# Four-layer graph network on one core: adding some gathered near rows on GpSimd between the gathers

## The chip, the core and the metric

The kernel runs on one core of one Trainium2 chip. The metric is the device time of one execution in microseconds (us); the figure given for a kernel is the median of its runs. A profiled execution has a time of its own and, a little shorter, a span from the first to the last instruction in the trace; all places in time below are microseconds from the start of that span.

Engines are named as in the profile: PE is TensorE (matrix products), DVE is VectorE, ACT is ScalarE, POOL is GpSimd, SP is SyncE (it only issues DMA transfers here).

## What is computed

There are N = 2708 nodes with D = 128 features and a dense adjacency matrix `adj`. Four layers follow one another, each on `h = relu(layernorm(x))`, each adding its result to `x`. The change lies in the second half of the first layer:

```python
d  = 1 / sqrt(sum(A, axis=-1))
z  = leaky_relu((d * (A @ (d * h))) @ W1 + b1, 0.1)     # first product with A
S  = exp(-sqrt(|z_i - z_j|^2 + 1e-10) / 2)              # all pairs of nodes
S  = where(rank of S in its row < 4, S, 0)              # four nearest of each node
A2 = S + A
d2 = 1 / sqrt(sum(A2, axis=-1))
x  = x + (d2 * (A2 @ (d2 * h))) @ W2 + b2               # second product
```

`S` has four nonzero entries in a row. So `A2 @ y` is the dense product `A @ y` plus, for each node, four rows of `y`, picked by index and weighed by `S`. Layer 1 is an attention layer that needs all of the new `x`; layers 2 and 3 are two more products with `adj`.

## The kernel before

**Tiles.** The nodes are cut into T = 22 tiles of 128 (the last has 20). `xs[:, t, :]` is tile t of `x`, 128 x 128 in float32, and stays in SBUF. `adj` comes in transposed; `chunk(i)` is a band of 128 of its rows, 1354 KB, loaded by SP's queue. GROUPS are the six groups of four tiles (the last has two); a group's 512 columns of a product fill one PSUM bank.

**Second product.** After the four nearest of each node are known (`top_i`, `top_v`), `y2 = dinv2 * (h @ W2)` is written to SBUF and to a table in HBM, `ydr`. Two things then run side by side.

- `aggregate(y2, done_l0, ...)` (line 388; matmuls recorded at L400) is the dense product. For the first 17 bands PE multiplies one band into all six banks while SP loads the next; the last five bands are kept in SBUF and are multiplied bank by bank, so that the banks become complete one after the other. For each of the first four complete banks `done_l0` runs `to_x1`: ACT copies the bank to `u2T` (L968), PE transposes it (L378), DVE scales it and adds it to `xs` (L962). Then `layernorm_relu` makes `h1` of the group. The last two groups, `E4` (tiles 16 to 19) and `E5` (tiles 20 and 21), are written out by hand below (`x1`, `moments`, `roots`, `scales`, `normed` and so on).
- The four near rows of every node are gathered from `ydr`. `gathered(idx)` (L918) issues one indirect DMA on POOL's queue: 128 indices, one row of 512 bytes for each partition, 64 KB. POOL works out its descriptors. There are 85 of them: four for each of the tiles 0 to 20, and one (`last_four`) for the 20 nodes of tile 21. The destination is one of 23 buffers `gath`. `add_near(t)` adds them: DVE does `xs[t] = gath * simd[t, k] + xs[t]`, once for each k (L929; L84 where the order is written by hand).

**Order.** Gathers stand on POOL in the order of the tiles, one after another. DVE's adds of the tiles 0 to 14 stand ahead of everything that `done_l0` does. Those of the tiles 15, 16, 17 and 18 stand in `done_l0` of the groups 0, 1, 2 and 3, behind that group's layernorm. Tile 19 (`T - 3`) follows by hand, then `x1(E4)` and `x1(E5)`. The four rows of tile 20 (`T - 2`) are weighed and added on POOL itself (L1029, L1030), behind the last gather:

```python
for g, k in zip(near_late[T - 2], range(TOPK)):
    pin(nc.gpsimd.tensor_scalar(g, g, simd[:, T - 2, k : k + 1], None, op0=ALU.mult))
    pin(nc.gpsimd.tensor_tensor(xs[:, T - 2, :], g, xs[:, T - 2, :], ALU.add))
```

`pin(...)` and the engines `pe`, `dve`, `act` keep instructions in the order of the program on their engine; other instructions are placed by a scheduler. Each engine works through its instructions in order, and one that waits holds up all behind it. `last_four` reaches `xs` of tile 21 by a small product with `four_w` (L1164 to L1170).

**What follows.** `x1(E5)` adds the dense part to the tiles 20 and 21; from there DVE and ACT go on to the layernorms of `E4` and `E5`, `rows_of`, the maximum `rmax` over all nodes and `w_n`. The whole next layer (masks, `total`) reads `rmax` or `w_n`.

Of the kernel before, what the change touches and what calls it, by code (L numbers as in the profile page):

```python
# [12 lines left out]
ALU = mybir.AluOpType  # L13
# [5 lines left out]
TOPK = 4  # L19
# [5 lines left out]
def kernel(  # L25
# [18 lines left out]
    nc = tc.nc  # L44
    N, D = x.shape
    assert D == P
    T = -(-N // P)
# [25 lines left out]
    def pin(ins):  # L73

        return tc.keep_in_program_order(ins)
# [10 lines left out]
    pe, dve, act = Ordered(nc.tensor), Ordered(nc.vector), Ordered(nc.scalar)  # L86
# [26 lines left out]
    def spread(y, queue):  # L113

        for g in range(1, 4):
            queue.dma_start(y[32 * g : 32 * g + TAIL, T - 1, :], y[:TAIL, T - 1, :])
# [16 lines left out]
    xs = keep.tile([P, T, D], F32, name="xs")  # L133
# [101 lines left out]
    with nc.allow_non_contiguous_dma(reason="256 elements"):  # L235
# [16 lines left out]
        out=above, in_=ones_b, pattern=[[1, P]], compare_op=ALU.is_ge, fill=0.0, base=-1, channel_multiplier=-1  # L252
# [17 lines left out]
    for v, first, fill in ((1, 3, float(P // 2)), (2, 2, -1e5)):  # L270
        nc.gpsimd.affine_select(
            out=empty[:, v, :], in_=empty[:, v, :], pattern=[[0, T]],
# [3 lines left out]
            out=empty[:, v, :], in_=empty[:, v, :], pattern=[[-PER, T]],  # L276
# [42 lines left out]
    def layernorm_relu(dst, g):  # L319

        t0, t1 = GROUPS[g]
        n = t1 - t0
        st = small.tile([P, 4, 6], F32, name="ln_st")
        mv = small.tile([P, 4, 2], F32, name="ln_mv")
        rs = small.tile([P, 4], F32, name="ln_rs")
        for t in range(t0, t1):
            nc.vector.bn_stats(st[:, t - t0, :], xs[:, t, :])
            nc.vector.bn_aggr(mv[:, t - t0, :], st[:, t - t0, :])
        root = nc.scalar.activation(rs[:, :n], mv[:, :n, 1], AF.Sqrt, bias=ln_eps)
        nc.vector.reciprocal(rs[:, :n], rs[:, :n])  # L330
        nm = small.tile([P, 4], F32, name="ln_nm")
        nc.vector.scalar_tensor_tensor(
            nm[:, :n], mv[:, :n, 0], -1.0, rs[:, :n], op0=ALU.mult, op1=ALU.mult
        )
        for t in range(t0, t1):
            o = t - t0
            nc.scalar.activation(
                dst[:, t, :],
                xs[:, t, :],
                AF.Relu,  # L340
                scale=rs[:, o : o + 1],
                bias=nm[:, o : o + 1],
            )
        return root
# [43 lines left out]
    def aggregate(y, done, more=None, kept=0, back=1, first=1):  # L388

        out = [acc(b) for b in range(NKB)]
        last = T - pools["n"]

        def product(i, b):
            k0, n = KBS[b]
            r = slice(32 * (b % 4), 32 * (b % 4) + TAIL) if i == T - 1 else slice(0, P)
            nc.tensor.matmul(  # L400
                out[b][:, :n],
                y[r, i, :],
                chunk(i)[r, k0 : k0 + n],
                start=(i == 0),
                stop=(i == T - 2),
            )

        for i in range(last):
            if more is not None:
                more(i)  # L410
            resident[i] = chunk(i)
            if i > 2 and T - 1 in resident and pools["apart"]:
                last_rows()
            for b in range(NKB):
                product(i, b)
            if i < last - kept:
                del resident[i]
            if i >= back and (i - back) % 2 == 0:
                absent = [j for j in range(last, T) if j not in resident]
                for j in absent[: first if i == back else 1]:  # L420
                    chunk(j)
        if more is not None:
            for i in range(last, T):
                more(i)
        for b in range(NKB):
            product(T - 1, b)
        for b in range(NKB):
            for i in range(last, T - 1):
                product(i, b)
            if b:  # L430
                done(b - 1, out)
        done(NKB - 1, out)
# [356 lines left out]
    for t in range(T):  # L789
# [4 lines left out]
        for bs in (range(4), range(4, NKB)):  # L794
# [7 lines left out]
            for b in bs:  # L802
                k0, n = KBS[b]
                g = 32 * (b % 4)
# [18 lines left out]
    near_u = res.tile([P, T, TOPK], U32, name="near_u")  # L823
# [33 lines left out]
    ydr = dram.tile([P * T, D], F32, name="ydr")  # L857
# [39 lines left out]
    simd = res.tile([P, T, TOPK], F32, name="simd")  # L897
# [6 lines left out]
    near_p = res.tile([P, 1], U32, name="near_p")  # L904
# [8 lines left out]
    nc.vector.tensor_tensor(four_w, four_w, ident[:, 64:96], ALU.add)  # L913
    nc.vector.tensor_tensor(four_w, four_w, ident[:, 96:128], ALU.add)

    def gathered(idx):
        g = res.tile([P, D], F32, name="gath", bufs=23)
        nc.gpsimd.indirect_dma_start(  # L918
            out=g[: idx.shape[0], :],
            out_offset=None,  # L920
            in_=ydr[:, :],
            in_offset=bass.IndirectOffsetOnAxis(ap=idx, axis=0),
        )
        return g

    def add_near(t, engine=nc.vector):
        for k in range(TOPK):
            g = gathered(near_u[:, t, k : k + 1])
            engine.scalar_tensor_tensor(  # L929
                xs[:, t, :],  # L930
                g,
                simd[:, t, k : k + 1],
                xs[:, t, :],
                op0=ALU.mult,
                op1=ALU.add,
            )
            engine = nc.vector if engine is nc.vector else dve

    def vec(name, n=T, dt=F32):
        return keep.tile([P, n], dt, name=name)
# [17 lines left out]
    def to_x1(g, s2):  # L966
        k0, n = KBS[g]
        nc.scalar.copy(u2T[:, k0 : k0 + n], s2[g][:, :n])  # L968
        node_product(u2T, None, g, add_l0)
# [4 lines left out]
    def terms(g):  # L974

        t0, t1 = GROUPS[g]
        k0, n = KBS[g]
        if not r_ps:
            r_ps.append(acc(0))
        transposed(hT, h1, g, nc.scalar.copy)  # L980
        p = ps_s.tile([P, 512], F32, name="ps")
        nc.tensor.matmul(p[:, :n], rep, hT[:, k0 : k0 + n], start=True, stop=True)
        nc.scalar.copy(row_all[:, k0 : k0 + n], p[:, :n])
        for t in range(t0, t1):
            nc.tensor.transpose(
                r_ps[0][: width(t), t : t + 1], row_all[:1, cols(t)], ident[:1, :1]
            )
        nc.vector.tensor_copy(r_nat[:, t0:t1], r_ps[0][:, t0:t1])
# [16 lines left out]
    def done_l0(g, s2):  # L1005
        if g >= NG - 2:
            complete.append(s2[g])
            return
        to_x1(g, s2)
        layernorm_relu(h1, g)  # L1010
        for t in late[g]:
            add_near(t, dve)
        if g:
            terms(g - 1)

    for t in range(15):
        add_near(t)
    aggregate(y2, done_l0, lambda i: spread(y2, nc.sync) if i == 4 else None, kept=4, back=5)

    E4, E5 = NG - 2, NG - 1

    near_late = {
        t: [gathered(near_u[:, t, k : k + 1]) for k in range(TOPK)] for t in (T - 3, T - 2)
    }
    last_four = gathered(near_p)
    for g, k in zip(near_late[T - 2], range(TOPK)):
        pin(nc.gpsimd.tensor_scalar(g, g, simd[:, T - 2, k : k + 1], None, op0=ALU.mult))  # L1029
        pin(nc.gpsimd.tensor_tensor(xs[:, T - 2, :], g, xs[:, T - 2, :], ALU.add))  # L1030
    for g, k in zip(near_late[T - 3], range(TOPK)):
        dve.scalar_tensor_tensor(
            xs[:, T - 3, :],
            g,
            simd[:, T - 3, k : k + 1],
            xs[:, T - 3, :],
            op0=ALU.mult,
            op1=ALU.add,
        )

    turned = []
    for g, s2 in zip((E4, E5), complete):
# [907 lines left out]
```

## Time and profile before

| | us |
|---|---|
| median of 15 runs | 1108.15 (1103.31 to 1119.15) |
| the profiled execution, its time | 1106.0 |
| its span | 1104.3 |
| first gather starts on POOL | 299.00 |
| last gather (`last_four`) starts | 404.48 |
| POOL's last add of tile 20 ends | 410.12 |
| PE busy, whole span | 995.6 (90%) |
| DVE busy | 582.8 (53%) |
| ACT busy | 401.3 (36%) |
| POOL busy | 209.1 (19%) |

An engine's busy time is an average over stages with different limits. Here only the stage from 291 to 425 matters: the second product, the gathers beside it, and the tail in which the last groups are finished. In a row of the trace's order of time the first two numbers are start and duration, and the bracket holds the idle time of the engine before it and what ended that.

### The profile page before, as it was taken

The numbers are of one execution on the slowest core, as the hardware profiler recorded it, in microseconds if no ns is written. First come the engines' busy times: TensorE is split into PE (matmuls) and PEld (weight loads), VectorE is DVE, ScalarE is ACT, GpSimd is POOL, SyncE is SP. The second block draws the span as 40 slices with busy tenths as digits, with TensorE's granted clock in tenths as the row PEclk, the third lists the DMA queues.
The fourth block names the chain that finished last, engine by engine and source line by source line (L and its number), as shares of the span: only waits on it lengthen the run. The fifth ranks groups of instructions, "written<-read, shape, count | busy, mean of one in ns | idle before, by whom it ended". The sixth has DMA issues, their size and how long they took to land.

```text
span 1104.3 us, 10114 instructions
## 1 busy us (share of the span) xinstructions
PE 995.6 (90%) x3551; PEld 487.6 (44%) x3551; DVE 582.8 (53%) x1185; ACT 401.3 (36%) x625; POOL 209.1 (19%) x199
## 2 busy tenths in 40 slices
PE   7999999999998998899787367777999999999998
PEld 5444444444343455454343133333444455455444
DVE  4365368999842267847466489998310321032003
ACT  6010045444300056668775288786200210021000
POOL 2000000000177760023333145551000000000000
PEclk9999999999998997899999769999999999999999
DMA  9987220004399525889999899999999257715811
GB/s 287 335 313 231 82 70 13 0 1 166 110 366 400 182 90 232 373 325 423 421 419 416 293 421 430 429 431 394 393 352 387 93 207 273 262 64 210 304 42 51
DMA packets 48995, 284.09 MB, mean 257 GB/s; under 512 B 6815, under 2 KB 18171, under 8 KB 29333
## 3 DMA queue, kind: packets, MB, share of 16 engines
q1 hardware_dynamic: 38191, 189.13, 45.6%
q0 software_dynamic: 10512, 94.32, 21.1%
q8 instruction: 28, 0.46, 0.2%
q14 instruction: 24, 0.19, 0.0%
q10 hardware_dynamic: 240, 0.00, 0.0%
HBM read 251.44 MB, written 33.00 MB: 258 GB/s over the span
## 4 chain that ended last, share of the span: by engine, by line
PE 67%; DMA 18%; DVE 8%; ACT 4%; issue 2%; POOL 0%; SPq 0%; DVEq 0%; POOLq 0%; ACTq 0%
PE acc L400 32%; PE acc L84 16%; PE acc L797 10%; DMA pair<-table,pair_u 8%; DMA mov<-in_adj_dram,src_u 5%; PE ps L84 4%; DVE att L84 3%; DMA chunk<-in_adj_dram 2%; PE ps L380 1%; ACT att L84 1%; DVE top_i L834 1%; DMA held<-in_adj_dram 1%; PE acc L805 1%; ACT sg L1510 1%; DVE mask L84 1%
## 5 line engine op out<-in xcount | busy, mean ns | idle before, releaser
L84 PE MATMUL acc<-att,xw 128*128 128x512 f32 (+2 forms) x264 | 110.2, 569 | 54.2 <-DVE att L84 54.1
L400 PE MATMUL acc<-chunk,h 128*128 128x512 f32 (+1 forms) x384 | 148.0, 542 | 0.0
L84 PE MATMUL acc<-mov,wt 128*128 128x512 f32 (+1 forms) x264 | 109.5, 561 | 18.4 <-DVE mov L84 18.2
L918 POOL DMA_INDIRECT gath<-ydr,near_u x84 | 79.9, 951 | 191.5 <-issue 179.6
L797 PE MATMUL acc<-zT 128*128 128x512 f32 (+2 forms) x264 | 112.3, 559 | 0.0
L400 PEld LDWEIGHTS acc<-chunk,h 128*128 128x128 f32 x384 | 68.8, 190 | 74.1 <-issue 74.1
L84 PEld LDWEIGHTS acc<-att,xw 128*128 128x128 f32 (+1 forms) x264 | 49.8, 196 | 114.6 <-issue 82.3
L400 PE MATMUL acc<-chunk,y 128*128 128x512 f32 x204 | 82.8, 568 | 7.9 <-DMA chunk<-in_adj_dram 7.1
L84 PEld LDWEIGHTS acc<-mov,wt 128*128 128x128 f32 x264 | 47.4, 191 | 79.8 <-DVE mov L84 45.9
L812 ACT COPY strip<-acc 128x512 f32<-128x512 f32 (+1 forms) x132 | 60.4, 558 | 59.2 <-issue 35.8
L1735 POOL DMA_INDIRECT pair<-table,pair_u x22 | 64.0, 2911 | 79.2 <-DVE att L84 44.7
L84 DVE SCALAR_TENSOR_TENSOR att<-pair,kap 128x2708 f32<-128x2708 f32 (+3 forms) x24 | 67.1, 2803 | 22.0 <-DMA pair<-table,pair_u 21.3
L84 DVE COPY mov<-knots 2x512 f32<-2x512 f32 x126 | 47.2, 399 | 50.7 <-DMA mov<-in_adj_dram,src_u 23.8
L400 PE MATMUL acc<-chunk,attended 128*128 128x512 f32 x192 | 73.1, 542 | 0.0
L84 ACT ACTIVATE att<-att,sca 128x2708 f32<-128x2708 f32 (+3 forms) x24 | 56.7, 2362 | 41.3 <-DVE att L84 41.3
L84 DVE SCALAR_TENSOR_TENSOR att<-row_all,inv_s,att 128x2708 f32<-128x2708 f32 (+3 forms) x24 | 67.2, 2798 | 4.0 <-ACT att L84 4.0
L814 DVE MAX8 top_v<-strip 128x8 f32<-128x2708 f32 (+1 forms) x22 | 64.6, 2964 | 7.3 <-ACT strip L812 7.3
L797 PEld LDWEIGHTS acc<-zT 128*128 128x128 f32 (+1 forms) x264 | 45.1, 185 | 51.3 <-issue 43.8
L400 PEld LDWEIGHTS acc<-chunk,y 128*128 128x128 f32 x204 | 38.4, 198 | 52.2 <-issue 47.4
L84 ACT ACTIVATE att<-att,hb 128x2708 f32<-128x2708 f32 (+3 forms) x24 | 56.7, 2364 | 0.8
L1510 ACT ACTIVATE sg<-row_all,c_nat 128x2708 bf16<-128x2708 f32 (+1 forms) x22 | 56.4, 2564 | 0.1
L84 ACT COPY knots<-acc 128x512 f32<-128x512 f32 x66 | 37.3, 595 | 40.5 <-PE acc L84 40.4
(355 smaller groups left out, 1244.4 us busy)
## 6 DMA issues: line engine op xcount, KB each, us to landing
chunk<-in_adj_dram SPq DMA_DIRECT2D x75, 1354.0 KB
table<-knots SPq DMA_DIRECT2D x19, 1354.0 KB
res<-in_adj_dram SPq DMA_DIRECT2D x9, 1354.0 KB
held<-in_adj_dram SPq DMA_DIRECT2D x11, 512.0 KB
held<-in_adj_dram SPq DMA_DIRECT2D x16, 256.0 KB
upper<-in_adj_dram SPq DMA_DIRECT2D x4, 842.0 KB
held<-in_adj_dram SPq DMA_DIRECT2D x3, 1024.0 KB
chunkY<-in_adj_dram SPq DMA_DIRECT2D x2, 1354.0 KB
```

What stands on the lines that cost most here:

```text
L84: return lambda *a, **k: pin(getattr(self.engine, name)(*a, **k))
L380: mm = nc.tensor.matmul(p[: width(t), t - t0, :], srcT[:, cols(t)], w, start=True, stop=True)
L400: nc.tensor.matmul(out[b][:, :n], y[r, i, :], chunk(i)[r, k0 : k0 + n], start=(i == 0), stop=(i == T - 2),)
L797: mm = nc.tensor.matmul(zz[b][:w, :n], zT[:, cols(t)], zT[:, k0 : k0 + n], start=True, stop=False)
L805: nc.tensor.matmul(zz[b][:w, :n], ones_b[g : g + 3, :w], sq_rows[g : g + 3, k0 : k0 + n], start=False, stop=True,)
L812: copied = nc.scalar.copy(s[:w, k0 : k0 + n], zz[b][:w, :n])
L814: nc.vector.max(top_v[:w, t, :], s[:w, :])
L834: pin(nc.vector.max_index(top_i[:w, t, :], top_v[:w, t, :], strips[t][:w, :]))
L918: nc.gpsimd.indirect_dma_start(out=g[: idx.shape[0], :], out_offset=None, in_=ydr[:, :], in_offset=bass.IndirectOffsetOnAxis(ap=idx, axis=0),)
L1510: nc.scalar.activation(sg[:w, :], row_all[:w, :], AF.Sign, bias=c_nat[:w, t : t + 1], accum_out=signs[:w, t : t + 1],)
L1735: nc.gpsimd.indirect_dma_start(out=r[:w].rearrange("p a n -> p (a n)"), out_offset=None, in_=table[:, :], in_offset=bass.IndirectOffsetOnA ...
```

## The change

Of each of the tiles 3 to 14, 16 and 18, the fourth near row is no longer added by DVE. For the tiles 3 to 14 (`SHARED`) ACT multiplies it by its weight in place, and POOL adds it to `xs`. For the tiles 16 and 18 (`ALONE`) POOL does both. POOL's part, `join`, is kept in the list `waiting` and is issued ahead of the fourth gather after the tile's own last one, so three gathers stand between the gather of a row and the add of it. All gathers and joins are pinned to the order of the program. The gathers of the tiles 15 to 20 and of tile 21 are now issued in the program ahead of `aggregate`; on POOL they stand in the same order as before. In all 14 adds (12 of `SHARED`, 2 of `ALONE`) leave DVE, 12 multiplications come to ACT, and 14 adds and 2 multiplications come to POOL. As recorded by the program, POOL has 19 gathers, the add of tile 3, four gathers, the add of tile 4, and so on. On ACT the 12 multiplications stand ahead of the first copy to `u2T`.

```diff
+    waiting = []
+
     def gathered(idx):
+        if waiting and waiting[0][0] <= 0:
+            waiting.pop(0)[1]()
+        for v in waiting:
+            v[0] -= 1
         g = res.tile([P, D], F32, name="gath", bufs=23)
-        nc.gpsimd.indirect_dma_start(
...
+        pin(
+            nc.gpsimd.indirect_dma_start(
...
-    def add_near(t, engine=nc.vector):
-        for k in range(TOPK):
-            g = gathered(near_u[:, t, k : k + 1])
+    SHARED, ALONE = range(3, 15), (16, 18)
+
+    def near_rows(t):
+        rows_ = [gathered(near_u[:, t, k : k + 1]) for k in range(TOPK)]
+        if t in SHARED or t in ALONE:
+            g, s_ = rows_.pop(), simd[:, t, TOPK - 1 : TOPK]
+            if t in SHARED:
+                nc.scalar.mul(g, g, s_)
+
+            def join():
+                if t in ALONE:
+                    pin(nc.gpsimd.tensor_scalar(g, g, s_, None, op0=ALU.mult))
+                pin(nc.gpsimd.tensor_tensor(xs[:, t, :], g, xs[:, t, :], ALU.add))
+
+            waiting.append([3, join])
+        return rows_
+
+    def add_near(t, rows_, engine=nc.vector):
+        for k, g in enumerate(rows_):
             engine.scalar_tensor_tensor(
                 xs[:, t, :],
                 g,
...
         for t in late[g]:
-            add_near(t, dve)
+            add_near(t, near_late[t], dve)
...
-    for t in range(15):
-        add_near(t)
+    near_late = {}
+    for t in range(T - 3):
+        rows_ = near_rows(t)
+        if t < 15:
+            add_near(t, rows_)
+        else:
+            near_late[t] = rows_
+    near_late.update((t, near_rows(t)) for t in (T - 3, T - 2))
+    last_four = gathered(near_p)
     aggregate(y2, done_l0, lambda i: spread(y2, nc.sync) if i == 4 else None, kept=4, back=5)
...
-    near_late = {
-        t: [gathered(near_u[:, t, k : k + 1]) for k in range(TOPK)] for t in (T - 3, T - 2)
-    }
-    last_four = gathered(near_p)
     for g, k in zip(near_late[T - 2], range(TOPK)):
         pin(nc.gpsimd.tensor_scalar(g, g, simd[:, T - 2, k : k + 1], None, op0=ALU.mult))
         pin(nc.gpsimd.tensor_tensor(xs[:, T - 2, :], g, xs[:, T - 2, :], ALU.add))
-    for g, k in zip(near_late[T - 3], range(TOPK)):
...
+    add_near(T - 3, near_late[T - 3], dve)
```

More of the change, by code (lines that the diff above doesn't have):

```diff
@@ L914 @@
     nc.vector.tensor_tensor(four_w, four_w, ident[:, 96:128], ALU.add)
+    waiting = []
     def gathered(idx):
+        if waiting and waiting[0][0] <= 0:
+            waiting.pop(0)[1]()
+        for v in waiting:
+            v[0] -= 1
         g = res.tile([P, D], F32, name="gath", bufs=23)
[L918 to L922, printed above, removed]
-        )
-        return g
-    def add_near(t, engine=nc.vector):
-        for k in range(TOPK):
-            g = gathered(near_u[:, t, k : k + 1])
+        pin(
+            nc.gpsimd.indirect_dma_start(
+                out=g[: idx.shape[0], :],
+                out_offset=None,
+                in_=ydr[:, :],
+                in_offset=bass.IndirectOffsetOnAxis(ap=idx, axis=0),
+            )
+        )
+        return g
+    SHARED, ALONE = range(3, 15), (16, 18)
[13 more added lines that the diff above has]
+        for k, g in enumerate(rows_):
             engine.scalar_tensor_tensor(
@@ L1011, in done_l0 @@
         for t in late[g]:
-            add_near(t, dve)
+            add_near(t, near_late[t], dve)
         if g:
             terms(g - 1)
-    for t in range(15):
-        add_near(t)
+    near_late = {}
[7 more added lines that the diff above has]
+    last_four = gathered(near_p)
+    assert not waiting
     aggregate(y2, done_l0, lambda i: spread(y2, nc.sync) if i == 4 else None, kept=4, back=5)
     E4, E5 = NG - 2, NG - 1
-    near_late = {
-        t: [gathered(near_u[:, t, k : k + 1]) for k in range(TOPK)] for t in (T - 3, T - 2)
-    }
-    last_four = gathered(near_p)
     for g, k in zip(near_late[T - 2], range(TOPK)):
@@ L1030 @@
         pin(nc.gpsimd.tensor_tensor(xs[:, T - 2, :], g, xs[:, T - 2, :], ALU.add))
-    for g, k in zip(near_late[T - 3], range(TOPK)):
[L1032 to L1039, printed above, removed]
+    add_near(T - 3, near_late[T - 3], dve)
     turned = []
```

## The prediction

> **What bounds the stage now.** I first asked the profile's page for the gathers and for PE's share of this product, because the change adds work between gathers.
>
> ```profile
> L918 POOL DMA_INDIRECT gath<-ydr,near_u x84 | 79.9, 951 | 191.5 <-issue 179.6
> L400 PE MATMUL acc<-chunk,y 128*128 128x512 f32 x204 | 82.8, 568 | 7.9 <-DMA chunk<-in_adj_dram 7.1
> ```
>
> The busy share of POOL (19% of the span) hides that POOL is full here. From the first gather's start (299.00) to the last one's (404.48) there are 84 steps in 105.48 us: 1.256 us each, of which 0.944 is the gather and 0.30 a gap that follows it. No gather waits longer than this gap for anything. PE, beside it, waited 7.1 us for bands of `adj`.
>
> Next I read the order of time at the end of the stage, POOL first and then DVE.
>
> ```profile
> 404.48 0.94 POOL L918 DMA_INDIRECT gath<-ydr,near_p  x1 [0.30 <-DVE ln_rs L330]
> 405.46 0.76 POOL L1029 TENSOR_SCALAR gath<-gath,simd 128x128 f32<-128x128 f32 x1
> 406.31 0.46 POOL L1030 TENSOR_TENSOR xs<-gath,xs 128x128 f32<-128x128 f32 x1
> ...
> 409.67 0.45 POOL L1030 TENSOR_TENSOR xs<-gath,xs 128x128 f32<-128x128 f32 x1
> ```
>
> ```profile
> 410.54 1.92 DVE L84 SCALAR_TENSOR_TENSOR xs<-gath,simd,xs 128x128 f32<-128x128 f32 x7
> 412.38 1.62 DVE L84 SCALAR_TENSOR_TENSOR xs<-ps,dinv,xs 128x128 f32<-128x128 f32 x6
> 413.93 0.85 DVE L84 BATCH_NORM_STATS2 ln_st<-xs 128x6 f32<-128x128 f32 x4
> ```
>
> POOL's last add of tile 20 ends at 410.12. The six adds of the dense part are `x1(E4)` (tiles 16 to 19) and `x1(E5)` (20 and 21), 0.27 each, so the one that needs POOL's result, tile 20, starts at 412.38 + 4 x 0.27 = 413.46. POOL has **3.3 us of slack**, and no more. Behind that add DVE has, in its fixed order, the moments, the scales, `rmax` and all that the next layer starts from; SP's next loads for that layer are issued only at 428.27, when PE has used up bands with `w_n`. So whatever delays tile 20 by more than 3.3 us moves the rest of the kernel.
>
> Last I read how long a gather takes to land, while SP loads bands (320 to 368) and when it no longer does (374 to 390): the DMA view of the two stretches. The last number is us from issue to landing.
>
> ```profile
> q1 hardware_dynamic: 1715, 16.50, 86.4%
> q0 software_dynamic: 1219, 2.49, 14.2%
> gath<-ydr,near_u POOLq DMA_INDIRECT x39, 6.0
> ```
>
> ```profile
> q0 software_dynamic: 398, 0.81, 17.7%
> gath<-ydr,near_u POOLq DMA_INDIRECT x14, 2.5
> ```
>
> The DMA engines are full up to about 368, and a gather then takes 6.0 us instead of 2.5. This is not a queue of gathers behind each other: the second gather, issued at 300.36 with one before it, already took 6.7 us, as soon as SP's loads had begun (300.48), and later ones stay near 6. Spacing the gathers should therefore not shorten it much.
>
> **What the change moves.** DVE loses 14 adds of 0.35 us. The 12 of the tiles 3 to 14 were hidden, since DVE is waiting for gathers then. The one of tile 18 is on DVE's path at 410 (0.27), but goes for nothing if POOL ends last. ACT gets 12 multiplications; the nearest row is ACT's scaling of `y2` at L863, 0.39 us for the same shape. ACT is idle there until 387.41.
>
> POOL gets the joins, and its order is fixed, so a join that waits holds back every gather behind it. Take a shared tile whose fourth gather is issued at time 0. Three more follow, and POOL reaches the join at 3 x 1.25 + 0.94 = 4.7. The row lands at 6.0 under load; ACT multiplies it (0.39), and I add 0.1 for the two hand-overs: ready at 6.5. POOL waits **1.8 us**. DVE's third add of the tile, which must come first as well, was gathered 1.25 earlier and takes 0.35, so it is done. When bands no longer load, the row is ready at 2.5 + 0.5 = 3.0 and POOL does not wait.
>
> The add itself is 0.46 on POOL (L1030). Behind it stands a gap that no row shows for an add followed by a gather: between 0.05 (as between POOL's operations after 405) and 0.30 (as between gathers); I take 0.15, halfway. In return the 0.30 gap before the next gather falls away. Net 0.46 + 0.15 - 0.30 = 0.31 for each join, plus its wait.
>
> How many wait? With a wait, four gathers and a join take 5.0 + 2.1 = 7.1 us. The first join is reached at 322.7 (it stands behind the gather issued at 321.74) and runs at 324.5; the following ones run at about 331.6, 338.7, 345.8, 352.9, 360.0 and 367.1. The seventh multiplies a row that was issued near 360.6, still under load; the eighth falls after it. So seven wait:
> - seven joins with a wait: 7 x (1.8 + 0.31) = 14.8 us;
> - five without: 5 x 0.35 = 1.75 (0.04 is lost before the add, as after the gather at 404.48);
> - tiles 16 and 18, with POOL's own multiplication (0.60) and a gap: 2 x 1.0 = 2.0.
>
> POOL's tail moves by 18.6 us, its last add ends at 428.7, and the end of the kernel moves by 18.6 - 3.3 = **15.3 us**.
>
> What else becomes late, and is covered by this: ACT's copies to `u2T` stand behind the multiplication of tile 14. Its row, issued at 373.3 before, now comes some 17 us later, lands near 393 and holds back the copy of 387.41 by about 5.5 us, and with it PE's transposes. DVE's adds of the tiles 16 and 18 follow their joins on POOL. The gathers of tile 19 land near 419. All this is over before 428.7; without POOL's delay as cover the copy alone would cost a few us.
>
> What is gained: four gathers in 7.1 us instead of 5.0 take 14.2% x 5.0 / 7.1 = 10.0% of the DMA engines, so loads run 4.2 / 86.4 = 4.9% faster, some 2.3 us over the 47 us in which they limit. PE's products may end that much sooner. Nothing comes of it, since POOL is last.
>
> The Trainium skill, "DMA: Bandwidth & Descriptors", section "Anatomy of one DMA", gives a transfer from GpSimd's queue as 2.0 us plus its bytes at 436 GB/s; for 64 KB that is an estimate of 2.15 us. The unloaded rows (2.5) come near, those under load (6.0) do not. By the rule every row is there before POOL reaches its join, nothing waits, and the sum is 0.31 to 0.35 for each of 12 joins plus 2.0: about 6 us on POOL, 2.6 at the end. The same page, section "SWDGE vs HWDGE vs iDMA", says that a DMA engine alternates between the queues packet by packet, which speaks for the longer time. I go by the rows.
>
> **Sum.** The profiled execution took 1106.0, so 1121.3 for such a one; it lies 2.15 under the median of 1108.15, which becomes 1123.5.
>
> Bounds. Downward: landing at 4.5, halfway between the two rows, leaves a wait of 0.4 and POOL moves by 7 to 10 (by the gap of 0.05 or 0.30): 4 to 7 at the end, 1112 to 1115. Upward: DVE's waits show single gathers that took 9 to 11 us (an add at 341.41 after 5.56 of waiting, of a gather issued at 330.58); if three joins meet such rows they wait 3 more each, and with the gap at 0.30 POOL moves by 25 to 27: 22 to 24 at the end, 1130 to 1132.
>
> **Rivals.**
> - *No wait at the joins.* Gathers that come less often meet emptier DMA queues, land in about 4.5 or less, and only the adds remain. For it: the skill's price, and 2.5 in the unloaded rows. Against: 6.7 for the second gather of all. End: +0.5 to +7, so 1109 to 1115.
> - *Not slower: bands arrive sooner and the joins fit into POOL's gaps.* The place is PE's waits for bands between 320 and 347. The price is the 2.3 us above; all 7.1 us at most. It decides only if POOL's tail moves by less than 3.3 us less whatever PE gains, for otherwise tile 20 is late all the same; even with joins at no cost, POOL's 85 gathers in a row allow no more than 3.3 us of gain. Since the net cost of 14 joins at the smallest gap is already 14 x 0.21 + 2 x 0.65 = 4.2, this needs gathers that become shorter when something stands between them, for which no row speaks. 1105 to 1108.
> - *More than that is lost.* Late rows as in the upper bound, or PE coming back at a lower clock after the longer pause (0.78 granted from 347 to 360, after its waits). 1131 to 1136.
>
> **Chances.** The forecast, 1116 to 1131: 0.72. No wait at the joins: 0.14, of which a third lies within 0.3%. Not slower: 0.08, half of it faster by over 0.3%. More lost: 0.06. A difference of 0.3% (3.3 us) is about what a measurement of this kernel tells from none. Faster 0.04, within 0.3% 0.09, slower 0.87. The range from 1111 to 1130 leaves out most of the not-slower case, the lower end of the no-wait case and the case of more loss.
>
> **What would show it.** In the changed profile seven of POOL's adds between 322 and 368 should stand behind about 2 us of idle time ended by ACT's `gath`, with gathers in groups of four, the last five behind none. The last gather should start near 423 and the last add of tile 20 end near 429, with DVE's add of the dense part of tile 20 directly behind it, ended by POOL. PE's waits for bands should shrink by 2 us or so. I am wrong if the adds come without waits, if the gathers' pace of 1.25 itself changes, or if DVE's add of tile 20 waits for something other than POOL.

## The result and the profile after

The changed kernel takes **1124.29 us** (median of 12 runs, 1120.04 to 1129.24). Beside it the kernel before took 1106.92 (62 runs). The ratio is 1.0158, with an interval of 1.0142 to 1.0174: 17.4 us slower. The profiled execution took 1123.04, with a span of 1121.3; before it was 1106.0 and 1104.3, so the two traces to be compared lie 17.0 us apart. Of these, 1.1 us is there before the stage begins (the first gather starts at 300.11 instead of 299.00) and is not the change's doing as far as can be seen: the kernels of the experiments below are the same up to there, and theirs starts between 296.03 and 300.18. Differences below are taken from the first gather on.

The page's groups first: the gathers, and PE's share of the dense product.

```profile
L925 POOL DMA_INDIRECT gath<-ydr,near_u x84 | 80.0, 953 | 189.4 <-issue 187.6
L400 PE MATMUL acc<-chunk,y 128*128 128x512 f32 x204 | 79.8, 551 | 5.7 <-DMA chunk<-in_adj_dram 4.9
```

The gathers themselves cost what they did (80.0 us for 84, before 79.9). PE is better off: its waits for bands fell from 7.1 to 4.9, and its products take 551 ns instead of 568. All the same the kernel is slower. Why is seen on POOL, in its order of time around the first and the seventh join and the first one behind the loads:

```profile
322.74 0.94 POOL L925 DMA_INDIRECT gath<-ydr,near_u  x1 [0.31 <-issue]
325.85 0.45 POOL L946 TENSOR_TENSOR xs<-gath,xs 128x128 f32<-128x128 f32 x1 [2.17 <-ACT gath L941]
...
367.73 0.45 POOL L946 TENSOR_TENSOR xs<-gath,xs 128x128 f32<-128x128 f32 x1 [1.82 <-ACT gath L941]
...
373.06 0.47 POOL L946 TENSOR_TENSOR xs<-gath,xs 128x128 f32<-128x128 f32 x1
```

The third gather behind the row has been issued at 322.74, and POOL then stands for 2.17 us until ACT has multiplied the row, because the row has not landed. While POOL stands, no gather is issued. The waits of the seven joins are 2.17, 1.72, 1.67, 1.56, 1.63, 1.63 and 1.82, together **12.2 us**. The add at 373.06 and the four after it wait for nothing. The stretch of DMA that lies under these waits (320 to 368; the last number is us from issue to landing):

```profile
q1 hardware_dynamic: 1795, 17.19, 88.4%
q0 software_dynamic: 957, 1.97, 11.2%
gath<-ydr,near_u POOLq DMA_INDIRECT x27, 5.9
```

27 gathers are issued here instead of 39, their share fell from 14.2% to 11.2%, and SP's loads moved 17.19 MB instead of 16.50. A gather nevertheless takes 5.9 us to land, before 6.0. Spacing the gathers did not make them land sooner.

The end of the stage, on POOL and then on DVE:

```profile
423.81 0.95 POOL L925 DMA_INDIRECT gath<-ydr,near_p  x1 [0.31 <-issue]
...
428.86 0.45 POOL L1050 TENSOR_TENSOR xs<-gath,xs 128x128 f32<-128x128 f32 x1
```

```profile
424.07 1.12 DVE L84 SCALAR_TENSOR_TENSOR xs<-ps,dinv,xs 128x128 f32<-128x128 f32 x4
429.35 0.60 DVE L84 SCALAR_TENSOR_TENSOR xs<-ps,dinv,xs 128x128 f32<-128x128 f32 x2 [4.16 <-POOL xs L1050]
```

From the first gather to the last it is 123.70 us, before 105.48: POOL's tail moved by **18.2 us**. DVE stood ready for tile 20 at 425.2 and waited 4.16 us for POOL; before it came to that add 3.3 us after POOL was done. On the chain that ended last POOL had 0% and now has 6%; the page's line before, and then now:

```profile
PE 67%; DMA 18%; DVE 8%; ACT 4%; issue 2%; POOL 0%; SPq 0%; DVEq 0%; POOLq 0%; ACTq 0%
```

```profile
PE 58%; DMA 21%; POOL 6%; DVE 6%; issue 5%; ACT 3%; SPq 0%; POOLq 0%; DVEq 0%; ACTq 0%
```

PE's order of time shows what the wider spacing did bring. PE waits for bands at three places: 2.26, 1.19 and 3.64 us before, 2.54, 0.73 and 1.63 now. The third wait and what follows it, before and then now:

```profile
346.95 34.88 PE L400 MATMUL acc<-chunk,y 128*128 128x512 f32 x84 [3.64 <-DMA chunk<-in_adj_dram]
381.76 9.04 PE L400 MATMUL acc<-res,y 20*128 20x512 f32 x28
```

```profile
345.73 32.04 PE L400 MATMUL acc<-chunk,y 128*128 128x512 f32 x84 [1.63 <-DMA chunk<-in_adj_dram]
377.70 9.04 PE L400 MATMUL acc<-res,y 20*128 20x512 f32 x28
```

PE begins the products of the kept bands (`res`) at 377.70, before at 381.76: 5.2 us sooner, measured from the first gather. 2.2 us are shorter waits. 2.8 us are the long row of 84 products, 32.04 instead of 34.88, and here it is the granted clock that differs (the share of its full speed that PE was given). Two rows of windows, 347 to 367, the kernel before and then the changed one; the number after the engines is the granted clock:

```profile
347.00:367.00 20.00, 20.00 (x45) 9.13 (x46) 5.68 (x17) 0.00 (x0) 15.10 (x16) 0.86 1.01 392
```

```profile
347.00:367.00 20.00, 20.00 (x54) 9.38 (x53) 3.17 (x9) 0.80 (x2) 12.46 (x15) 1.00 1.01 406
```

In the kernel before the granted clock was half for 6.8 us from 345.8, in its wait of 3.64 us and behind it; after the wait of 1.63 it stayed full. But none of the 5.2 us can arrive. ACT's first copy to `u2T` stands behind the multiplication for tile 14 and runs at 392.55 (before 387.41), and tile 20 waits for POOL in any case.

At `rmax`, on which the next layer depends, the kernel is 14.8 us late (15.9 less 1.1), before and then now:

```profile
423.66 0.29 DVE L84 TENSOR_REDUCE rmax<-acc 128x1 f32<-128x128 f32 x1 [1.11 <-PE acc L84]
```

```profile
439.60 0.29 DVE L84 TENSOR_REDUCE rmax<-acc 128x1 f32<-128x128 f32 x1 [1.11 <-PE acc L84]
```

About 1.1 us more is lost between there and the end. In this tail PE has gaps and its granted clock is half for a while. These windows, before and after:

```profile
414.10:427.80 13.70, 10.78 (x52) 8.00 (x56) 9.45 (x48) 8.66 (x17) 0.00 (x0) 0.50 0.25 100
```

```profile
418.40:442.30 23.90, 9.47 (x45) 6.86 (x47) 11.41 (x50) 7.80 (x17) 8.99 (x14) 0.50 0.24 93
```

PE is busy for 10.78 us of the first and 9.47 of the second, and the half clock lasts 10.2 us longer. That this is where the 1.1 us went fits, but was not tested by itself.

### The profile page after: what moved, and what is told of

It is laid out like the page before. It is cut to its first block, busy times and chain, and to the rows that moved or that the text cites. A ratio compares the mean times of both kernels' runs of the same rounds, so it can differ in the third digit from the quotient of the medians.

```text
span 1121.3 us, 10087 instructions
## 1 busy us (share of the span) xinstructions
PE 999.2 (89%) x3551; PEld 488.9 (44%) x3551; DVE 579.5 (52%) x1171; ACT 406.2 (36%) x637; POOL 217.1 (19%) x215
## 4 chain that ended last, share of the span: by engine, by line
PE 58%; DMA 21%; POOL 6%; DVE 6%; issue 5%; ACT 3%; SPq 0%; POOLq 0%; DVEq 0%; ACTq 0%
PE acc L400 26%; PE acc L84 15%; DMA pair<-table,pair_u 11%; PE acc L797 10%; DMA mov<-in_adj_dram,src_u 5%; POOL gath L925 5%; PE ps L84 4%; DMA gath<-ydr,near_u 3%; DVE att L84 2%; PE ps L380 1%; DMA held<-in_adj_dram 1%; PE acc L805 1%; DVE mask L84 1%; ACT att L84 1%; DVE mov L84 1%
## 5 line engine op out<-in xcount | busy, mean ns | idle before, releaser
L400 PE MATMUL acc<-chunk,y 128*128 128x512 f32 x204 | 79.8, 551 | 5.7 <-DMA chunk<-in_adj_dram 4.9
```

The lines of the kernel that those rows point to most:

```text
L400: nc.tensor.matmul(out[b][:, :n], y[r, i, :], chunk(i)[r, k0 : k0 + n], start=(i == 0), stop=(i == T - 2),)
```

## Experiments

The theory: joins that stand three gathers behind their row wait for it, POOL's in-order queue hands each wait on to all later gathers, and whatever exceeds POOL's 3.3 us of slack moves the kernel. The rivals: the fixed order of the gathers costs it, without any join (A); the adds themselves cost it, waits or not (B); ACT's copies, held back by the multiplication of tile 14, would set the end without POOL too (C); wider spacing is worth nothing to PE (D). Every difference is taken against the kernel before on the same chip.

### The order alone, and a chip on which PE is slow

**pinned** keeps the pinned order of the gathers and drops all joins. **later** puts seven gathers between a row and its join. **loaded** joins the tiles 3 to 9 alone, **unloaded** the rest alone.

```diff
-    SHARED, ALONE = range(3, 15), (16, 18)
+    SHARED, ALONE = (), ()                      # pinned
+    SHARED, ALONE = range(3, 10), ()            # loaded
+    SHARED, ALONE = range(10, 15), (16, 18)     # unloaded
...
-            waiting.append([3, join])
+            waiting.append([7, join])           # later
```

> The changed kernel with no tile in SHARED or ALONE: all adds are DVE's again, only the place of the late gathers in the program and their pinning remain. Theory: POOL's order is the same as before, so no difference within 1 us. Rival (the new program order, the scheduler or the buffers cost something): several us slower.

> Each join stands seven gathers behind its row instead of three, so POOL reaches it 9.7 us after that row's issue; rows land in 6.0 us or so under load and ACT needs 0.5 more. Theory (waits at the joins are most of the loss): no join waits, each costs POOL 0.34 (tiles 3 to 14) or 1.2 (tiles 16, 18), 6.5 us in all, and the end moves by 6.5 - 3.3 = 3.2 us against the kernel before, 14 us less than the change. Rival (the adds on POOL, or ACT's and DVE's new hand-overs, cost by themselves): the loss stays near 17 us.

> Joins of the tiles 3 to 9 alone, the seven that waited. Theory: POOL's tail moves by 13.9 us (as the gather behind the seventh join did), less 3.3 us of slack: 10.6 us slower than before. PE's products end some 5 us sooner, since ACT's last multiplication is done near 367 and no longer holds back the copies to u2T, and this is worth nothing because POOL is last. Rival (PE and ACT held up by the multiplications set the end): close to the kernel before, or faster.

> Joins of the tiles 10 to 14, 16 and 18 alone, which did not wait. Theory: 5 x 0.34 + 2 x 1.2 = 4.1 us on POOL, 3.3 of it slack: 0.8 us slower, hardly to be told from none. Rival (POOL has no such slack, each us on POOL is a us at the end): 4 us slower.

Measured, as ratios to 1177.29 us of the kernel before, with their intervals: pinned 1.0006 [0.9993, 1.0019], later 1.0027 [1.0007, 1.0047], unloaded 1.0022 [1.0005, 1.004], loaded 0.9747 [0.9728, 0.9765]. The four ran on a chip on which the kernel before itself takes 70 us more than elsewhere, and the trace of `pinned`, which is as slow, says where. A row of windows and, from 356 on, PE's order of time:

```profile
340.00:360.00 20.00, 6.46 (x8) 2.01 (x7) 4.91 (x15) 0.00 (x0) 15.12 (x17) 0.50 0.33 114
```

```profile
356.60 1.01 PE L400 MATMUL acc<-chunk,y 128*128 128x512 f32 x1 [1.78 <-issue]
359.41 1.01 PE L400 MATMUL acc<-chunk,y 128*128 128x512 f32 x1 [1.80 <-issue]
...
414.70 34.40 PE L400 MATMUL acc<-chunk,y 128*128 128x512 f32 x84 [0.30 <-issue]
```

From about 327 to 414 PE gives one product in about 2.8 us: 1.0 us of work at a granted clock of 0.50, and a pause of 1.8 for which no releaser is found. POOL has time to spare there; its order of time in `pinned` at the last gather of tile 20:

```profile
462.07 0.94 POOL L925 DMA_INDIRECT gath<-ydr,near_u  x1 [59.99 <-DVE xs L84]
```

POOL waits 60 us for a buffer, which comes free only with DVE's adds behind PE's banks, so up to 60 us spent on joins before that place can't be seen at the end. In `later` and `unloaded` POOL does not wait there, but it is through at 421.8 and 417.9, while DVE stands until 462 and 461 for PE's first bank. What these runs can say: the pinned order costs nothing measurable there (A could be hidden by the same waits, so this alone does not rule it out; the unchanged pace of 1.25 between gathers does), and in `later` none of the twelve joins of `SHARED` waits (the add of tile 16 stood 4.01 us, for a release that the trace does not name). That `later` came out 2.8 us slower, near the 3.2 expected, is luck as far as can be seen: POOL was through some 40 us before DVE's wait ended. The question of the end had to be asked elsewhere, with the three kernels that follow.

`loaded` was 31 us faster there, which no theory expected. In its trace the slow stretch does not begin at 327: PE is busy for 15.1, 19.8 and 20.0 us of the three windows of 20 us from 320 on, in `pinned` for 9.7, 6.5 and 7.5. Its seven joins waited 1.0 to 2.35 us each. But it stands elsewhere: PE waits 32.33 us for ACT's first copy to `u2T`, which starts only at 421.27, for a release that the trace does not name; a half clock of 34.1 us, from 392.3, falls mostly into this wait. Why the stretch did not set in and this wait did was not settled, and the changed kernel itself was not run on that chip.

### Seven gathers between the row and its join (later_2)

The edit of `later`, against rival B.

> The kernel of the first run of this name again, because there the kernel before took 1177 us and PE gave out one product in 2.8 us for some 85 us, so that nothing on POOL could be last. Where the kernel before takes about 1107: theory (waits at the joins are most of the loss): no join waits, 6.5 us on POOL, 3.3 of it slack, so 3.2 us slower than before. Rival (the adds on POOL, or the hand-overs to ACT and DVE, cost by themselves): some 17 us slower, as the change.

Measured: 1113.02, ratio 1.0067 [1.0042, 1.0093]: 5.9 us slower instead of 17.4. POOL's order of time around a join, and at the end:

```profile
325.86 0.95 POOL L925 DMA_INDIRECT gath<-ydr,near_u  x1 [0.30 <-issue]
326.82 0.47 POOL L946 TENSOR_TENSOR xs<-gath,xs 128x128 f32<-128x128 f32 x1
327.45 0.95 POOL L925 DMA_INDIRECT gath<-ydr,near_u  x1 [0.16 <-issue]
...
415.38 0.60 POOL L1049 TENSOR_SCALAR gath<-gath,simd 128x128 f32<-128x128 f32 x1 [0.82 <-DMA gath<-ydr,near_u]
```

No join waits. From gather to gather with a join between it is 1.59 us instead of 1.256: **0.34 for a join that does not wait**. Twelve of these are 4.0, and the two tiles of `ALONE` cost 1.2 each: 6.4. POOL's tail moved by 6.4. The waits, not the adds, were two thirds of the change's cost. B holds for most of the remaining third: 14 adds in a full queue exceed its slack of 3.3 even without a wait.

The kernel lost more than 6.4 - 3.3 = 3.1, though, and the last line shows something new: tile 20's last row lands late and POOL waits 0.82 for it. PE is 4.3 us sooner here, so SP's first loads for the next layer begin sooner (405.70 and 407.71, before 409.23 and 411.25) while the gathers end later, and the two meet.

### The joins under load alone, and the others alone (loaded_2, unloaded_2)

The edits of `loaded` and `unloaded`. In `loaded_2` tile 14 has no multiplication and ACT's copies are free, which tests C.

> The joins of the tiles 3 to 9 alone again, where the kernel before takes about 1107. Theory: POOL's last gather starts 13.9 us later after its first one than before; less 3.3 of slack the end moves by 10.6, and by some 1.4 more if the next stage loses as much after the longer pause as it did with the later joins: 10.6 to 12 us slower. PE's products end some 5 us sooner and this is worth nothing. Rival (ACT's multiplications in front of its copies set the end in the change; with none after 367 the loss is gone): within 2 us of before.

> The joins of the tiles 10 to 14, 16 and 18 alone again, where the kernel before takes about 1107. Theory: no join waits, 4.1 us on POOL, 3.3 of it slack: 0.8 us slower, up to 3 if the last gathers now meet SP's next loads near 409 and land late, as those of the kernel with later joins did. Rival (there is no slack): 4 us or more.

`loaded_2`: 1120.31, ratio 1.0113 [1.0084, 1.0142], 12.8 us. Seven waits of 12.5 in all and 7 x 0.31 make 14.7; the tail moved by 14.6. The first copy to `u2T` ran at 383.75, held by nothing, and DVE still waited for POOL:

```profile
425.56 0.59 DVE L84 SCALAR_TENSOR_TENSOR xs<-ps,dinv,xs 128x128 f32<-128x128 f32 x2 [4.17 <-POOL xs L1050]
```

With free copies three quarters of the loss remain, and POOL's tail less its slack of 3.3 makes 11.3 of these 12.8: C falls as a cause of this result.

`unloaded_2`: 1114.18, ratio 1.0059 [1.0038, 1.0081], 6.6 us. This was a miss; I had counted on no wait at all. POOL's order of time at the first two joins (tiles 10 and 11), and at tile 20:

```profile
358.37 0.45 POOL L946 TENSOR_TENSOR xs<-gath,xs 128x128 f32<-128x128 f32 x1 [1.69 <-ACT gath L941]
...
365.28 0.59 POOL L946 TENSOR_TENSOR xs<-gath,xs 128x128 f32<-128x128 f32 x1 [1.61 <-ACT gath L941]
...
415.56 0.60 POOL L1049 TENSOR_SCALAR gath<-gath,simd 128x128 f32<-128x128 f32 x1 [0.67 <-DMA gath<-ydr,near_u]
```

Two joins wait after all. With the seven earlier joins gone, the rows of the tiles 10 and 11 are gathered while SP still loads bands; in the changed kernel it was the delay by the other seven that had carried them behind the loads. The sum with that: 3.3 of waits, 2 x 0.31, 3 x 0.35 and 2 x 1.2 make 7.4; the tail moved by 7.8. At tile 20 POOL waited 0.55 and 0.67 more for rows that met SP's loads (406.49 and 408.51).

### Spacing where POOL is not last (short_none, short_loaded)

Against D: work of the late tiles is left out, so that POOL's tail sets nothing. The near rows of the tiles 10 to 21 are not added, those of 15 to 21 not gathered (the small product for tile 21 goes too; its lines are not printed here). Both kernels are shortened alike and do not compute the whole result; `short_loaded` then has the seven joins of `loaded`.

```diff
-    SHARED, ALONE = range(3, 15), (16, 18)
+    SHARED, ALONE = (), ()                      # short_none
+    SHARED, ALONE = range(3, 10), ()            # short_loaded
...
-    for t in range(T - 3):
+    for t in range(15):
         rows_ = near_rows(t)
-        if t < 15:
+        if t < 10:
...
-    near_late.update((t, near_rows(t)) for t in (T - 3, T - 2))
-    last_four = gathered(near_p)
+    near_late.update((t, []) for t in range(15, T - 1))
...
```

> No joins, and POOL's late work is taken away so that POOL can't be last: the near rows of the tiles 10 to 21 are not added (those of 10 to 14 are still gathered, those of 15 to 21 are not gathered). Base for the next kernel. Both theories: DVE's path loses eight adds of 0.27 and more, so 2 to 4 us faster than the kernel before.

> The same work left out, but with the joins of the tiles 3 to 9, so gathers are spaced as in the change while bands load, and POOL is not last. Theory (the spacing speeds PE up, but POOL's own delay eats it): PE's products end about 5 us sooner, as they did in the change, and the kernel is 4 to 5 us faster than the one without joins. Rival (the spacing gains nothing at the end even where POOL is not last): no difference.

Measured: short_none 1104.82, ratio 0.9971 [0.9949, 0.9992]; short_loaded 1100.75, ratio 0.9941 [0.9916, 0.9965]. PE's first product with `res`, without joins and with them:

```profile
379.61 9.04 PE L400 MATMUL acc<-res,y 20*128 20x512 f32 x28
```

```profile
376.55 9.04 PE L400 MATMUL acc<-res,y 20*128 20x512 f32 x28
```

PE is 3.1 us sooner with the spaced gathers, and the medians lie 4.1 apart. The intervals of the two ratios overlap a little, and the spans of the two traces differ by only 1.3; but the runs of the two kernels themselves lie 3.2 apart in the mean, with an interval of 1.0 to 5.4. The joins of `short_loaded` waited as everywhere (1.56 to 2.03 us). So D falls: spaced gathers do let the bands come sooner, and some of that reaches the end where POOL is not last.

### A change that uses the gain (two_dve, three_dve, two_late)

Two or three joins only, and tile 20's rows are added by DVE instead of POOL, so that POOL's tail is shorter. `two_late` also holds back SP's two loads for the next layer, by a one-element write of DVE into their buffers that stands behind tile 20's adds.

```diff
-    SHARED, ALONE = range(3, 15), (16, 18)
+    SHARED, ALONE = (3, 4), ()                  # two_dve and two_late; three_dve: (3, 4, 5)
...
-    for g, k in zip(near_late[T - 2], range(TOPK)):
-        pin(nc.gpsimd.tensor_scalar(g, g, simd[:, T - 2, k : k + 1], None, op0=ALU.mult))
-        pin(nc.gpsimd.tensor_tensor(xs[:, T - 2, :], g, xs[:, T - 2, :], ALU.add))
...
+    add_near(T - 2, near_late[T - 2], dve)      # ahead of x1(E5)
+    early_at = [lay.tile([P, N], F32, name="chunk" + v, tag=v) for v in "YU"]   # two_late
+    for c in early_at:                                                          # two_late
+        dve.memset(c[:1, :1], 0.0)                                              # two_late
...
-            c = lay.tile([P, N], F32, name="chunk" + tag, tag=tag)
+            c = early_at[n] if n < 2 else lay.tile([P, N], F32, name="chunk" + tag, tag=tag)   # two_late
```

> A version that may beat both: joins of the tiles 3 and 4 alone (4.2 us on POOL, in the part where PE waits for bands), and the rows of tile 20 are added by DVE between the dense adds of the groups 4 and 5 instead of by POOL, which frees POOL of 4.6 us at its end for 1.1 us on DVE. Theory: PE gains 1 to 2 us, POOL is just not last, 0 to 1 us faster than before. Rival (POOL has no such room): 2 to 4 us slower.

> The same with the joins of the tiles 3, 4 and 5: 6.3 us on POOL, its last gather of tile 20 lands near 412, and DVE needs it at 413.5 less PE's gain. Theory: PE gains 2 to 3 us, of which about 1 is left after DVE's 1.1 and the late row: within 1 us of the kernel before. Rival: 4 us slower.

`two_dve`: 1110.29, ratio 1.0021 [1.0002, 1.004]. `three_dve`: 1110.22, ratio 1.0032 [1.0003, 1.0061]. Neither is faster, and by the medians both forecasts missed. DVE's order of time in `two_dve`:

```profile
414.43 0.35 DVE L84 SCALAR_TENSOR_TENSOR xs<-gath,simd,xs 128x128 f32<-128x128 f32 x1 [2.33 <-DMA gath<-ydr,near_u]
416.14 0.35 DVE L84 SCALAR_TENSOR_TENSOR xs<-gath,simd,xs 128x128 f32<-128x128 f32 x1 [1.35 <-DMA gath<-ydr,near_u]
```

The last row of tile 20 was issued at 408.96 and landed at 416.05, after 7.1 us. SP's loads had begun at 407.01 and 409.03. In `three_dve` they began at 403.5, and DVE waited 3.81 us for rows of tile 19. PE's gain thus starts the next layer's loads sooner, and these slow the very gathers on which the end depends. `two_late` takes that away:

> The version with the joins of the tiles 3 and 4 and tile 20 on DVE, with one edit more: SP's first two loads for the next layer wait for two one-element writes by DVE behind its last near row. In the version without it these loads started at 407 to 409 and the last gathers took 7.1 us to land instead of 2.5. Theory (that meeting is what spoiled the version): the last gathers land in 2.5, DVE's dense add of tile 20 comes 4 us sooner, 3 to 4 us faster than that version, so 0 to 1.5 us faster than the kernel before. Rival (the loads are needed at 409): as slow as that version or slower.

```profile
406.92 1.51 DVE L84 SCALAR_TENSOR_TENSOR xs<-gath,simd,xs 128x128 f32<-128x128 f32 x4
408.37 0.06 DVE L84 MEMSET chunkY<- 1x1 f32 x1
...
408.48 0.60 DVE L84 SCALAR_TENSOR_TENSOR xs<-ps,dinv,xs 128x128 f32<-128x128 f32 x2
```

The four rows are added without a wait, the loads begin at 408.51, and tile 20's dense add comes 2.0 us sooner than before (both measured from the first gather: 112.45 and 114.46). The time is 1107.19, ratio 0.9998 [0.9977, 1.0019]. In the traces tile 20's dense add is 4.0 us sooner than in `two_dve`, so the meeting with the loads did hold it back there; the intervals of the two ratios overlap. The 2.0 us are still there at `rmax` and gone at the end. That the loads, the first of which starts some 2 us later than before (again from the first gather on), take them back is likely, but was not tested. No version that computes the whole result beats the kernel before.

## Why the prediction was right, step by step

- **POOL is full and its order binds.** Held. The pace of the gathers is unchanged, and every wait of a join shows in the last gather.
- **Seven joins wait 1.8 us each.** Seven waited, 1.74 in the mean. Landing under load was put at 6.0 and is 5.9. The Trainium skill's price for a transfer on GpSimd's queue ("DMA: Bandwidth & Descriptors", section "Anatomy of one DMA"), an estimate of 2.15 us here, comes near the unloaded gathers (2.5 from 386 to 402) and not the loaded ones. Had the rows landed that soon, no join would have waited; `later_2`, in which none waits, lies 11.3 us below the changed kernel by the two medians.
- **The gap behind an add is 0.15.** It is 0.15 to 0.16; a join without a wait is 0.34, forecast 0.35.
- **The tiles 16 and 18 cost 1.0 each.** 1.2: the gather behind them is longer (up to 1.12 us).
- **POOL moves by 18.6, the slack is 3.3, the end moves by 15.3.** 18.2, and 14.8 at `rmax`; the median moved by 17.4. That the time itself (1124.29) lies 0.8 us from the forecast 1123.5 is in part luck: the forecast started from 1108.15, the median of 15 runs, and 62 runs put the kernel before at 1106.92. Up to `rmax` the sum fits the other kernels too, once POOL's waits for the rows of tile 20 are added:

| kernel | POOL's tail | less 3.3 | waits for tile 20's rows | late at `rmax` | median against before | interval of that |
|---|---|---|---|---|---|---|
| changed | 18.2 | 14.9 | 0 | 14.8 | +17.4 | 15.7 to 19.3 |
| loaded_2 | 14.6 | 11.3 | 0.5 | 11.7 | +12.8 | 9.3 to 15.7 |
| unloaded_2 | 7.8 | 4.5 | 1.2 | 5.6 | +6.6 | 4.2 to 9.0 |
| later_2 | 6.4 | 3.1 | 0.8 | 3.9 | +5.9 | 4.6 to 10.3 |

- **The terms that were missing.** The prediction has SP's next loads issued only at 428.27. That misses two: `chunkY` and `chunkU` go out at 409.23 and 411.25 in the kernel before, and where POOL's tail is later the last gathers meet them. This is the column of the waits for tile 20's rows. With it the sum comes within 0.1 us of the delay at `rmax` in all four traces. The rest, 1.0 to 2.6 us by the medians, is lost behind `rmax`, where the prediction put nothing. The half clock of the tail lasts longer there (13.7 us before; 20.5 in `later_2`, 23.9 in the other three), but how much of the loss is due to it, and how much is chance, stays open.
- **The upper bound.** It took a wait of DVE as a gather that lands after 9 to 11 us. The trace of the kernel before does not list every landing; the longest that it lists in this stretch takes 7.1 us.
- **PE's products end 2.3 us sooner and nothing comes of it.** Mis-sized: 5.2. The shorter waits were foreseen (2.2); that the half clock behind the third wait would go too (2.8) was not, though the prediction itself quotes 0.78 granted from 347 to 360. Nothing came of it, as said.
- **ACT's copy is held back to about 393.** 392.55.
- **The rivals.** "No wait at the joins" fell by the seven waits. "Not slower" needed more than POOL's slack allowed; the gain it named exists, but only in the shortened kernels does it get through. "More than that is lost" did not come about: no join of the changed kernel waited over 2.17 us, and behind its third wait for a band PE's clock was full where it had been half. In the tail it was half for longer, but the time stayed under 1131.

## What to carry to other kernels

In an engine's queue that is full, an operation that needs another engine's or a DMA's result costs its wait as well as its own duration, and everything behind it pays: multiply by the number of such operations and compare with the slack of the last item in the queue. Place it by the landing time under the load of that stage (here 5.9 us, not 2.5), and count in steps of the queue how far behind that is. When something is gained on another engine, look at what it starts sooner, for that can collide with the transfers that now end later (here 7.1 us for a row instead of 2.5).

## What was not expected of the hardware

- On one chip PE gave a product of 128x512 only every 2.8 us or so for some 85 us of this stage, at a granted clock of 0.50, in three of the four variants traced there, and not in `loaded`. (Of the kernel before only the time is known there, as long as theirs.) The Trainium skill ("TensorE: Matmul & The Clock Gate", section "Seeing it yourself") says that the clock's events in a profile have been unreliable on trn2, and that the gate has been seen stuck at a quarter rate for 50 us and more. Here the rows show a half rate, and 1.8 of each 2.8 us are a pause between products, by PE's order of time: a slow clock alone does not make that. What does stays open.
- The half clock comes in stretches of 3.4 us: 3.4, 6.8, 13.7, 20.5, 23.9 and 34.1 us were seen. That is the length of the window that the same page gives in Part 1 for the gate. The length of a wait does not by itself tell whether one follows: behind a wait of 2.14 us in `unloaded_2` 24 products took 11.02 us, behind one of 2.75 in `two_late` they took 9.32. So the 2.8 us that PE gained in the changed kernel came with a wait shorter by 2.0 us, but need not come with it every time.
- A gather of 64 KB issued beside two loads of 1354 KB took 7.1 us to land, against 2.5 alone.
